# Second layer of a two-layer decoder: three stages issued one after the other, or in turns

## The chip, the core and the metric

The kernel runs on one core of a Trainium2 chip. The metric is the device time of one execution in microseconds (us). A core has engines that run side by side and each work off their own queue of instructions: TensorE (PE in the profile; its weight loads have a row of their own, PEld), VectorE (DVE), ScalarE (ACT), GpSimd (POOL), and SyncE (SP), which here only issues transfers. Matmul results land in PSUM, a memory of eight banks; VectorE and ScalarE read it, GpSimd doesn't in this kernel. Everything else lives in SBUF, with 128 partitions.

## What is computed

The input `x` is 64 sequences of 64 tokens with 256 features, so 4096 tokens; `ctx_512` gives 64 context vectors of 64 features for each sequence. There are two layers of three residual blocks, each behind a layer norm. The first layer (a state-space scan, an attention, a mixture of experts) stays as it is. The change is to the second:

```python
x = x + _L1_attn_ref(_layernorm(x), ...)             # recurrent mean ("wkv")
x = x + _L1_xattn_ref(_layernorm(x), ctx_512, ctx_512)   # grouped attention ("gqa")
x = x + _L1_ffn_ref(_layernorm(x), ...)              # grouped experts ("ffn")
```

The recurrent mean mixes each token with the one before it in three ways, multiplies by three matrices, and runs a recurrence along the 64 tokens of a sequence:

```python
mfo = max(mx, kt + tf);  e1 = exp(mx - mfo);  e2 = exp(kt + tf - mfo)
out = (e1 * num + e2 * vt) / (e1 * den + e2)
mfs = max(mx + td, kt);  e1s = exp(mx + td - mfs);  e2s = exp(kt - mfs)
carry = (e1s * num + e2s * vt, e1s * den + e2s, mfs)
...
return sigmoid(rec @ Wr) * out @ Wo
```

The grouped attention has 32 query heads of 8 features over 8 key-value heads, within one sequence. The grouped experts choose 8 of 64 small experts for each token, gather their weights in 8 groups, add a mask term to the input of each group, and apply a gated pair of matrices (256 to 176) and one back (176 to 256) for each group; the eight results are summed.

No token depends on a token of another sequence, so all three stages can be done for one part of the sequences before another part is begun.

## The kernel before

The 4096 tokens are 8 blocks (`NBLK`) of 512 tokens (`TB`), which is 8 sequences (`NB`) or 4 tiles (`NT`) of 128 tokens. `x_sb` holds all of `x` in SBUF, 32 tiles of 128 x 256, and every stage adds its result to it in place. `run` goes through six phases, each over all 8 blocks: state-space scan, attention, experts, recurrent mean, grouped attention, grouped experts. Each phase has its own weight pool, work pool and PSUM pool; the pools lie in turn on the left and the right side of SBUF, so that the next phase's weights are loaded while one phase runs.

`phase` (L1114) is the loop of the last three phases: the front of a block is a function or a generator cut into pieces by `yield`; the items of a block then pass through a list of stages, each one step behind the one before, so that the stages of different items overlap. The order in which the program makes its instructions is what the queues start from. A framework then sorts them into the engines' queues and adds the waits; VectorE, ScalarE and GpSimd may get an instruction whose inputs are there ahead of an earlier one that still waits.

- Collecting (L696, `moe_collect`). The experts of the first layer leave two rows for each token in memory; an indirect transfer that GpSimd issues adds 128 rows to one tile of `x_sb`, 8 such transfers for a block. Blocks 0 and 1 are collected after the expert phase, the others one by one during the recurrent mean.
- Recurrent mean. `wkv_front` (L728): statistics of the layer norm, the norm on GpSimd (L106), transposes (L115), difference to the previous token (`wk_d`, L742), three mixes (`wk_mix`, L748), three projections into PSUM tiles of two banks (L755), copies and a sigmoid on ScalarE. `wkv_scan` (L766): three scans along the tokens on VectorE (L783, L801, L802), the exponents between them on VectorE, GpSimd and ScalarE, a reciprocal (`wk_dn`, L807), and the closing products on GpSimd (L808 to L812). `wkv_out` (L815): the output matrix and the addition to `x_sb`. All of it works on whole blocks: 128 partitions x (2 halves of the features x 512 tokens). Two PSUM tiles of two banks and four of one bank are in use.
- Grouped attention. `gqa_front` loads the context and lays it out for keys and values; `gqa_queries`, `gqa_max`, `gqa_turn`, `gqa_weights`, `gqa_values`, `gqa_out` treat one tile of 128 tokens each. All eight banks form one ring (tag `mm`).
- Grouped experts. `ffn_front` (9 pieces; L1012 to L1064): norm, transposes, the router matmul (`pl`), softmax, the largest 8, transposed weights (`weT`), the gathered weights (`pf`), a second softmax over the members of a group (`fl`, `soft`), and its transpose `smT`. `prep_ffn` (L985) makes the mask term's matrix once. An item is half of the groups of one tile: `ffn_up` (four `gu` tiles of one bank each, L1078 and L1082, then Silu on ScalarE, L1086, and a product on VectorE, L1087), `ffn_turn` (transposes, L1099, L1100), `ffn_down` (L1108), the addition to `x_sb` and the transfer of the result out.

ScalarE evaluates a function from a table that is loaded before it. The recurrent mean uses Exp and Sigmoid, the grouped attention Exp, the grouped experts Silu, and Exp in their front.

Of the kernel before, what the change touches and what calls it, by code (L numbers as in the profile page):

```python
# [6 lines left out]
F32 = mybir.dt.float32  # L7
# [11 lines left out]
NB = TB // S  # L19
NBLK = 8  # L20
# [21 lines left out]
class Net:  # L42
# [28 lines left out]
    def mm(self, shape, name):  # L71

        return self.pp.tile(shape, F32, tag="mm", bufs=8 - 2 * self.n_big, name=name)
# [5 lines left out]
    def open_psum(self, n_big):  # L79
        self.n_big = n_big  # L80
        self.pp = self.tc.alloc_tile_pool(name="psum", bufs=1, space=PSUM, reuse_waits="tile")


    def stats(self, wk, blk):

        nc = self.nc
        st = wk.tile([P, NT, 6], F32, tag="ln_st", bufs=2, name="ln_st")
        mv = wk.tile([P, NT, 2], F32, tag="ln_mv", bufs=2, name="ln_mv")
        for t in range(NT):
            nc.vector.bn_stats(st[:, t], self.x[:, blk * NT + t])  # L90
            nc.vector.bn_aggr(mv[:, t], st[:, t])
        ve = wk.tile([P, NT], F32, tag="ln_ve", bufs=2, name="ln_ve")
        nc.vector.tensor_scalar(ve, mv[:, :, 1], LN_EPS, None, ALU.add)
        rs = wk.tile([P, NT], F32, tag="ln_rs", bufs=2, name="ln_rs")
        nc.gpsimd.tensor_tensor(rs, ve, self.mhalf, ALU.pow)
        return mv, rs

    def neg_mean_times(self, wk, mv, rs, tag="ln_nm"):
        nm = wk.tile([P, NT], F32, tag=tag, bufs=2, name=tag)
# [19 lines left out]
    def ln_T(self, wk, blk, eng):  # L119
        nc = self.nc  # L120
        mv, rs = self.stats(wk, blk)
# [59 lines left out]
    def ssm_front(self, wk, w, blk):  # L181
        nc, te = self.nc, self.nc.tensor
        mv, rs = self.stats(wk, blk)
# [287 lines left out]
    def moe_front(self, wk, w, b, f):  # L471
# [6 lines left out]
        mv, rs = self.stats(wk, b)  # L478
# [169 lines left out]
    def moe_phase(self, wk, w):  # L648
# [40 lines left out]
        for b in range(2):  # L689
            self.moe_collect(b)  # L690

    def moe_collect(self, b):

        for k in range(2):
            for i in range(NT):
                self.nc.gpsimd.indirect_dma_start(self.x[:, b * NT + i], None, self.ys,  # L696
                                                  bass.IndirectOffsetOnAxis(self.left[:, b, k, i:i + 1], 0), compute_op=ALU.add)


    def w_wkv(self, side):  # L700
# [12 lines left out]
        w["tdp"] = wp.tile([P, 2, NB, S + 1], F32, name="wkv_tdp")  # L713
# [6 lines left out]
    def wkv_padded(self, wk, n, fill, bufs=1):  # L720

        t = wk.tile([P, 2, NB, S + 1], F32, tag="wk_" + n, bufs=bufs, name="wk_" + n)
        t = t.rearrange("p c b s -> p (c b) s")
# [3 lines left out]
    def wkv_plain(self, wk, n, bufs=1):  # L727
        t = wk.tile([P, 2, TB], F32, tag="wk_" + n, bufs=bufs, name="wk_" + n)  # L728
        return t, t.rearrange("p c (b s) -> p (c b) s", s=S)

    def wkv_front(self, wk, w, blk):
        nc, te, v, gp = self.nc, self.nc.tensor, self.nc.vector, self.nc.gpsimd
        mv, rs = self.stats(wk, blk)
        nm = self.neg_mean_times(wk, mv, rs)
        h = self.norm(wk, blk, rs, nm, gp)
        ps = self.transposed(h)
# [515 lines left out]
```

## Time and profile before

| | us |
|---|---|
| median of 3 runs | 2495.43 |
| lowest and highest run | 2490.35, 2496.96 |
| the profiled execution, by its own clock | 2489.17 |
| its span, first to last instruction | 2487.4 |
| TensorE busy (share of the span) | 2061.0 (83%) |
| VectorE busy | 1243.2 (50%) |
| ScalarE busy | 720.4 (29%) |
| GpSimd busy | 857.1 (34%) |

Busy time is the union of an engine's instructions. A matmul's end is modelled, so a busy TensorE need not be at its peak; the distance from one matmul to the next is the better measure of what one costs. "PEclk" is the TensorE clock that was granted, as a share of the full one. All times on the axis are counted from the first instruction. A share over the whole span is a mean over six phases with different limits, so the phases have to be looked at one by one.

### The profile page before, as it was taken

What the parts mean: (1) busy time and instruction counts of PE and PEld (TensorE: products, weight loads), DVE (VectorE), ACT (ScalarE), POOL (GpSimd) and SP (SyncE); (2) the same over time, 40 slices, a digit from 0 to 9 for tenths busy, and PEclk for the clock granted to TensorE, in tenths of its full rate; (3) what the DMA queues carried; (4) which work ended last, traced back from release to release, by engine and by line L of the source; (5) the groups of instructions that cost most, each with busy time, mean ns of one, the idle gap of its engine ahead of it and who ended that gap; (6) DMA issues with size and microseconds to landing.
All of it is one profiled execution on the core that took longest, in us unless ns stands there. A gap on an engine that the chain in (4) does not pass through costs nothing.

```text
span 2487.4 us, 31746 instructions
## 1 busy us (share of the span) xinstructions
PE 2061.0 (83%) x12394; PEld 1447.3 (58%) x12394; DVE 1243.2 (50%) x2672; ACT 720.4 (29%) x1282; POOL 857.1 (34%) x1001
## 2 busy tenths in 40 slices
PE   6899998999999479999822353538997999999999
PEld 3566674666667367888711121225764666667666
DVE  5554657544345433333325599886875323332322
ACT  2232431222232343333202122214662222222221
POOL 4443354222221432011289967656632000000000
PEclk8898999999999579999966676668997999999999
DMA  4011009540000111677333100022000000000000
GB/s 131 30 30 30 1 1 283 177 124 5 1 5 8 60 55 55 218 237 237 116 52 46 26 0 0 0 74 57 13 3 1 9 7 7 9 7 9 7 7 11
DMA packets 109960, 133.78 MB, mean 54 GB/s; under 512 B 31850, under 2 KB 98546, under 8 KB 109810
## 3 DMA queue, kind: packets, MB, share of 16 engines
q1 hardware_dynamic: 94482, 104.48, 13.7%
q0 software_dynamic: 15328, 27.27, 4.4%
q8 instruction: 98, 1.61, 0.3%
q14 instruction: 52, 0.43, 0.1%
HBM read 75.23 MB, written 56.49 MB: 53 GB/s over the span
## 4 chain that ended last, share of the span: by engine, by line
PE 32%; issue 13%; POOL 10%; DVE 7%; DMA 0%; SPq 0%; ACT 0%; POOLq 0%; DVEq 0%; ACTq 0%
PE gu_ps L1078 12%; PE acc L1108 6%; POOL x_sb L696 4%; PE gu_ps L1082 2%; PE aT_ps L1099 2%; DVE wk_dn L807 2%; PE st L919 2%; DVE wk_mix L748 1%; PE sc L906 1%; PE pq L883 1%; PE pv L930 1%; POOL moe_ys L646 1%; POOL h L106 1%; POOL wk_o L812 1%; DVE wk_den L801 1%
## 5 line engine op out<-in xcount | busy, mean ns | idle before, releaser
L1078 PE MATMUL gu_ps<-ffn_gu,hT 128*128 128x352 f32 x1024 | 315.5, 461 | 0.0
L1078 PEld LDWEIGHTS gu_ps<-ffn_gu,hT 128*128 128x128 f32 x1024 | 192.4, 191 | 97.2 <-issue 0.8
L1087 DVE SCALAR_TENSOR_TENSOR a<-a,fr_sca,gu_ps 128x176 f32<-128x176 f32 x256 | 84.6, 393 | 308.3 <-ACT a L1086 308.3
L115 PE MATMUL hT_ps<-ident,h 128*128 128x128 f32 x192 | 41.7, 356 | 177.8 <-POOL h L106 151.4
L1108 PE MATMUL acc<-ffn_d,aT 128*128 128x256 f32 x704 | 162.4, 379 | 0.0
L1086 ACT ACTIVATE a<-gu_ps 128x176 f32<-128x176 f32 x256 | 60.5, 322 | 348.0 <-PE gu_ps L1082 348.0
L106 POOL TENSOR_SCALAR h<-x_sb,ln_rs,ln_nm 128x256 f32<-128x256 f32 x64 | 44.8, 798 | 300.6 <-PE hT_ps L1012 298.2
L209 PE MATMUL proj<-hT,w_in 128*128 128x512 f32 x320 | 145.8, 612 | 0.0
L115 PEld LDWEIGHTS hT_ps<-ident,h 128*128 128x128 f32 x192 | 29.6, 176 | 190.0 <-POOL h L106 162.0
L1108 PEld LDWEIGHTS acc<-ffn_d,aT 128*128 128x128 f32 x704 | 128.8, 190 | 14.9
L392 POOL TENSOR_TENSOR p<-p,sm 128x1024 f32<-128x1024 f32 x32 | 60.9, 1902 | 186.1 <-DVE sm L391 186.1
L628 DVE TENSOR_TENSOR gT<-gT,uT 128x512 f32<-128x512 f32 x54 | 37.4, 692 | 166.9 <-ACT gT L627 166.9
L413 PE MATMUL po<-xa_vo,ctxT 128*128 128x256 f32 x512 | 117.6, 379 | 0.0
L696 POOL DMA_INDIRECT x_sb<-moe_ys,left x64 | 109.7, 1714 | 20.1 <-issue 19.8
L373 PE MATMUL q_ps<-hT,xa_q 128*128 128x512 f32 x256 | 113.8, 602 | 1.5 <-ACT hT L126 1.4
L413 PEld LDWEIGHTS po<-xa_vo,ctxT 128*128 128x128 f32 x512 | 96.3, 190 | 25.8 <-issue 12.2
L646 POOL DMA_DIRECT2D moe_ys<-y x38 | 27.2, 717 | 238.3 <-DVE y L645 231.3
L209 PEld LDWEIGHTS proj<-hT,w_in 128*128 128x128 f32 x320 | 61.4, 196 | 71.7 <-issue 68.6
L90 DVE BATCH_NORM_STATS2 ln_st<-x_sb 128x6 f32<-128x256 f32 x192 | 75.1, 405 | 42.2 <-DMA x_sb<-moe_ys,left 37.3
L755 PE MATMUL pk<-wk_mix,wkv_k 128*128 128x512 f32 x64 | 44.5, 850 | 54.5 <-DVE wk_mix L748 54.5
L254 POOL TENSOR_TENSOR ul<-ssm_U,la 128x512 f32<-128x512 f32 x32 | 34.1, 1067 | 156.8 <-PE pld L256 156.8
L540 POOL DMA_INDIRECT moe_hs<-moe_h,moe_slots x64 | 62.4, 974 | 73.5 <-issue 34.3
(324 smaller groups left out, 4587.8 us busy)
## 6 DMA issues: line engine op xcount, KB each, us to landing
moe_hs<-moe_zero SPq DMA_DIRECT2D x30, 1088.0 KB, 11.2
pack<-in_moe_pack_dram SPq DMA_DIRECT2D x38, 770.0 KB, 5.5
ht<-moe_hs SPq DMA_DIRECT2D x38, 272.0 KB, 2.8
moe_ys<-y POOLq DMA_DIRECT2D x38, 256.0 KB, 5.6
c<-in_ctx_dram SPq DMA_DIRECT2D x40, 128.0 KB, 3.0
x_sb<-in_x_dram SPq DMA_DIRECT2D x8, 512.0 KB, 7.3
out_dram<-x_sb SPq DMA_DIRECT2D x32, 128.0 KB, 1.7
ffn_gu<-in_ffn_guT_dram SPq DMA_DIRECT2D x8, 352.0 KB, 7.6
```

The lines of the kernel that those rows point to most:

```text
L90: nc.vector.bn_stats(st[:, t], self.x[:, blk * NT + t])
L106: eng.tensor_scalar(h[:, t], self.x[:, blk * NT + t], rs[:, t:t + 1], nm[:, t:t + 1], ALU.mult, ALU.add)
L115: self.nc.tensor.transpose(ps[:, t * P:(t + 1) * P], h[:, t, c * P:(c + 1) * P], self.ident)
L209: te.matmul(ps, w["in"][:, c, col:col + P], hT[:, c], start=c == 0, stop=c == 1)
L373: te.matmul(ps, wq[:, c, hp * P:(hp + 1) * P], hT[:, c], start=c == 0, stop=c == 1)
L392: nc.gpsimd.tensor_mul(p, p, bc(sm, 2, S))
L413: self.nc.tensor.matmul(po, st["cT"][:, hp], w["vo"][:, hp], start=hp == 0, stop=hp == 7)
L540: s = gp.indirect_dma_start(w["hs"], bass.IndirectOffsetOnAxis(w["slots"][:, b, k, i:i + 1], 0), ha[k][:, i], None).ins
L696: self.nc.gpsimd.indirect_dma_start(self.x[:, b * NT + i], None, self.ys, bass.IndirectOffsetOnAxis(self.left[:, b, k, i:i + 1], 0), compu ...
L1078: te.matmul(ps, f["hT"][:, c, tok], w["gu"][:, 4 * q + j, c], start=c == 0, stop=False)
L1087: v.scalar_tensor_tensor(a[:, e], a[:, e], f["sca"][:, k:k + 1], pg[j][:, 176:352], ALU.mult, ALU.mult)
L1108: self.nc.tensor.matmul(f["acc"][t], st["aT"][:, k], w["d"][:, k], start=k == 0, stop=k == 10)
```

## The change

The last three phases become one, `layer1`, with one PSUM pool: a ring of seven one-bank tiles (`n_mm = 7`) and one bank for the sums of `ffn_down` (tag `acc`). `beside` takes one piece at a time from several generators, in proportion to the numbers given with them, until all are done. After the recurrent mean of block 0 alone, and that of block 1 beside the attention of block 0, eight rounds follow: the grouped experts of block b, the recurrent mean of block b+2 (with the collecting of block b+3 ahead of it), and the grouped attention of block b+1 with the front of its experts behind it.

```diff
+        def wkv(b):
+            if b + 1 < NBLK:
+                yield from self.collect_block(b + 1)
+            if b < NBLK:
+                yield from self.wkv_block(wk, w_wkv, b)
+        def gqa(b):
+            if b < NBLK:
+                yield from self.gqa_block(wk, w_gqa, b)
+                yield from self.ffn_front(wk, w_ffn, b, fs[b])
+        def beside(*streams):
+            at = [0.0] * len(streams)
+            live = [iter(s) for s, _ in streams]
+            most = max(n for _, n in streams)
+            while any(x is not None for x in live):
+                for i, (_, n) in enumerate(streams):
+                    at[i] += n / most
+                    while at[i] >= 1 and live[i] is not None:
+                        at[i] -= 1
+                        if next(live[i], 1) is not None:
+                            live[i] = None
+        for _ in self.collect_block(0):
+            pass
+        beside((wkv(0), 1))
+        beside((wkv(1), 50), (gqa(0), 36))
+        self.prep_ffn(wk, w_ffn)
+        for b in range(NBLK):
+            beside((self.ffn_block(wk, w_ffn, b, fs), 40), (wkv(b + 2), 50), (gqa(b + 1), 40))
```

The recurrent mean works on half blocks (`HB`, 4 sequences, 2 tiles). `wkv_block` takes pieces of the scan of one half and of the front of the next half by turns. The norm moves from GpSimd to ScalarE, the projections use one bank each, the Sigmoid becomes an Exp whose 1 + e^-r is multiplied into the denominator, so that one reciprocal gives both, and many products overwrite their input:

```diff
-    def wkv_front(self, wk, w, blk):
+    def wkv_front(self, wk, w, n0, f):
...
-        h = self.norm(wk, blk, rs, nm, gp)
-        ps = self.transposed(h)
+        h = wk.tile([P, 2, D], F32, tag="wk_h", bufs=1, name="wk_h")
+        for t in range(2):
+            nc.scalar.activation(h[:, t], self.x[:, n0 + t], AF.Identity, bias=nm[:, t:t + 1], scale=rs[:, t:t + 1])
+        yield
+        ps = self.mm([P, 2 * HB, S], "wk_hT")
...
-            ps = self.big([P, 2, TB], "p" + n)
+            ps = self.mm([P, 2, HB * S], "p" + n)
...
-        nc.scalar.activation(r, proj("r", mixed(2))[0], AF.Sigmoid)
+        nc.scalar.activation(er, proj("r", mr)[0], AF.Exp, scale=-1.0)
...
-        gp.tensor_mul(ev[:, :, 1:], e2s[:, :, 1:], vs)
-        v.tensor_tensor_scan(flat(num), flat(e1s), flat(ev), 0.0, ALU.mult, ALU.add)
...
-        v.reciprocal(dn, dn)
-        gp.tensor_mul(ov, e1, num[:, :, :S])
-        gp.tensor_mul(e2, e2, vs)
-        gp.tensor_add(ov, ov, e2)
-        gp.tensor_mul(rv, rv, dn)
-        gp.tensor_mul(ov, ov, rv)
+        gp.tensor_mul(e2s[:, :, 1:], e2s[:, :, 1:], vs)
+        dn = den[:, :, :S]
+        v.tensor_mul(dn, dn, e1)
+        v.tensor_add(dn, dn, e2)
+        v.scalar_tensor_tensor(dn, er, 1.0, dn, ALU.add, ALU.mult)
+        yield
+        v.tensor_tensor_scan(flat(num), flat(e1s), flat(e2s), 0.0, ALU.mult, ALU.add)
+        gp.tensor_mul(e2, e2, vs)
+        yield
+        v.reciprocal(er, dn)
+        gp.tensor_mul(e1, e1, num[:, :, :S])
+        gp.tensor_add(e1, e1, e2)
+        yield
+        gp.tensor_mul(ov, e1, er)
...
+        v.tensor_add(self.x[:, n0:n0 + 2], self.x[:, n0:n0 + 2], po)
```

The pieces of the attention and of the experts come from generators of their own. The experts' pipeline runs on from one block to the next; `ffn_up` is cut between its second and third bank; `ffn_turn` takes small tiles of its own (three buffers); `ffn_front` has a cut more. To make room, many SBUF tiles have one buffer where they had two to four (context, keys, values, `soft`, the front's scratch), and the mask weights are loaded into a work tile in `prep_ffn`.

```diff
+        for k in range(b * n, (b + 1) * n + (len(stages) - 1 if b == NBLK - 1 else 0)):
+            for d, stage in enumerate(stages):
+                if 0 <= k - d < NBLK * n:
+                    c, i = divmod(k - d, n)
+                    yield from stage(wk, w, fs[c], c, i, self.fst[k - d])
...
-            f["acc"][t] = self.mm([P, D], "acc")
+            self.acc = self.pp.tile([P, D], F32, tag="acc", bufs=1, name="acc")
...
+        w[5] = self.w_ffn("left")
+        self.open_psum(0)
+        self.n_mm = 7
+        wk = self.pool("work3", "left")
+        self.layer1(wk, w[3], w[4], w[5])
```

The weights of the recurrent mean and of the attention are loaded, and the attention's tiles cleared on GpSimd, before the first layer's experts instead of after them; the grouped experts' weights follow right behind those experts.

## The prediction

> **What bounds the kernel now.** First the busy times by stage, in stretches of time that I cut where one phase hands over to the next (length, then busy us and instructions of each engine, the granted clock, the transfers' share, GB/s):
>
> ```profile
> core 0: us, PE busy (x) PEld busy (x) DVE busy (x) ACT busy (x) POOL busy (x), PEclk, DMA share, GB/s
> 1231.00:1268.00 37.00, 2.83 (x14) 2.14 (x12) 7.95 (x20) 0.00 (x0) 31.66 (x32) 0.60 0.40 57
> 1268.00:1674.00 406.00, 169.86 (x384) 87.64 (x384) 291.97 (x242) 87.39 (x89) 308.88 (x208) 0.67 0.14 23
> 1674.00:1690.00 16.00, 2.41 (x10) 2.16 (x11) 9.22 (x50) 1.09 (x2) 11.38 (x33) 0.54 0.88 213
> 1690.00:1870.00 180.00, 174.85 (x3512) 123.15 (x3510) 138.46 (x282) 106.98 (x199) 97.59 (x301) 0.99 0.07 15
> 1870.00:1895.00 25.00, 10.39 (x40) 8.20 (x41) 17.88 (x86) 2.00 (x4) 11.01 (x17) 0.50 0.00 0
> 1895.00:2487.40 592.40, 589.12 (x2874) 408.74 (x2872) 173.51 (x524) 146.60 (x385) 13.90 (x23) 1.00 0.02 8
> ```
>
> The second layer takes half of the span, from 1231 on. Its recurrent mean (second row) needs TensorE for a part of its 406 us, at 0.67 of the clock; VectorE and GpSimd carry it. Attention (fourth row) and experts (last) are TensorE's alone; GpSimd has nearly nothing to do beside the experts. The two kinds of stage run one after the other.
>
> Then the groups of the recurrent mean's stretch, to see what its cadence is made of (busy us, mean ns of one, idle before it and who ended it):
>
> ```profile
> L748 DVE SCALAR_TENSOR_TENSOR wk_mix<-wk_d,wkv_vec,wk_hp 128x512 f32<-128x512 f32 x48 | 55.6, 1208 | 34.2 <-POOL wk_d L742 31.7 <-PE pk L755 2.5
> L807 DVE RECIPROCAL wk_dn<-wk_dn 128x1024 f32<-128x1024 f32 x8 | 52.3, 6540 | 0.0
> ...
> L812 POOL TENSOR_TENSOR wk_o<-wk_o,wk_r 128x1024 f32<-128x1024 f32 x8 | 29.1, 3635 | 0.6
> ...
> L801 DVE TENSOR_TENSOR_SCAN wk_den<-wk_e1s,wk_e2s 128x1040 f32<-128x1040 f32 x8 | 24.4, 3044 | 5.8 <-ACT wk_e1s L797 5.8
> ```
>
> In the chain of waits the long reciprocals begin at 1420.09, 1451.10, 1492.31, 1536.81, 1577.88, 1622.29 and 1654.92: 39 us a block.
>
> Last, TensorE in order of time where the experts' first front stands alone:
>
> ```profile
> 1875.91 3.25 PE L1018 MATMUL pl<-ffn_r,hT 128*128 128x64 f32 x14 [1.04 <-DVE hT L1013]
> 1885.17 1.06 PE L1036 MATMUL weT_ps<-ident,fr_sc 128*64 128x128 f32 x4 [6.01 <-DVE fr_sc L1032]
> 1886.90 1.97 PE L1042 MATMUL pf<-ffn_at,fr_weT 64*128 64x64 f32 x8 [0.67 <-ACT fr_weT L1038]
> 1894.15 1.11 PE L1062 MATMUL smT_ps<-ident,ffn_soft 128*128 128x128 f32 x4 [5.29 <-DVE ffn_soft L1057]
> 1895.06 5.27 PE L1078 MATMUL gu_ps<-ffn_gu,hT 128*128 128x352 f32 x14
> ```
>
> The `gu` matmuls need `hT`, which the `pl` matmuls before them had read, and all PSUM was free; yet they stand behind `smT_ps`. TensorE keeps the order of issue when an input is late. VectorE doesn't: in the same 25 us its row has 86 instructions, most of them layer-norm statistics of later blocks slipped in between. This decides what the turns can hide.
>
> **What the skill says.** "Perfetto Trace Analysis", Optimization Strategy, says that where the most-contended engine changes over time, interleaving those regimes may help: rows two and six are such a pair. "ScalarE: Activation LUTs", What ACT_TABLE_LOAD costs, gives about 1283 ns for a change of function set plus a drain; the trace's loads take 1283 ns each, and it shows no separate drain. "SBUF — State Buffer", Who interferes with whom, says that a VectorE instruction with two SBUF inputs and a GpSimd instruction that reads SBUF block each other whole; here the 48 mixes average 1208 ns, while their median is 740, so it agrees. "TensorE: Matmul & The Clock Gate", Part 1, has the clock halved when TensorE idles; the rows agree (0.50 where it waits, 1.00 where it doesn't).
>
> **The change, part by part.** All times count against the profiled execution: 2489.17 us, of which 2487.4 is the span and 1.8 lies around it; the median of the runs is 6.3 above it.
>
> *TensorE's work.* It is nearly the same, now at full clock. Experts: 1895.06 to the last addition's start at 2484.2, 589 us, of which a whole block with its front takes 74.1 (`gu` groups at 1973.82 and 2047.91 in the chain). Attention: 174.9 less 11.05 for `mgu` is 163.8, 20.5 a block. Recurrent mean, a block: 48 projection matmuls of 256 columns at 0.231 (row L1108, 162.4/704), 16 of the output at the same, 8 transposes at 0.149 (L1099, 52.4/352): 11.1 + 3.7 + 1.2 = 16.0. A full round needs 74 + 20.5 + 16 = 110.5 us.
>
> *The other engines in a round.* VectorE: recurrent mean, each half 6 mixes, 6 exponent steps at 0.42 (256 columns, row L131), 3 scans at 1.2 and a reciprocal at 3.3 (halves of 2.31, the shortest scan, and 6.54), 4 products of 512 at 0.68, statistics 1.3, so 16 and 32 a block; attention 138.5/8 = 17; experts 173.5/8 = 22. Sum 71, and by the stretch that the recurrent mean shows (292 busy where its durations at their minimum sum to about 219) up to 95. GpSimd: 16 products of 512 at 1.07 (L254), 8 collects at 1.85, attention 97.6/8 = 12, norm 3: 47. ScalarE: attention 13, experts 18, recurrent mean 12, and table loads: by the turns Silu and Exp change about 10 times a round, against two or three loads a block in the experts now: 10 x 1.28 = 13, sum 56. All lie beside 110 of TensorE. Nothing is lost on them unless TensorE waits for one.
>
> *The lead-in.* Collecting ends 1246 for block 0 and 1261 for block 1, for these 16 transfers come first on GpSimd; now 17 clearing instructions, which move ahead of the experts, come before the first `rs` (1268.5). I take 1262. First half of block 0, alone: front 10 us, scan 19 (the durations above in a row), done at 1291; each further half by the cadence of 39 us a block plus fixed costs, 21: 1312 for block 0 and 1354 for block 1. The attention of block 0 fits beside it (20.5 of TensorE). Of the front behind it some 18 of the 23.7 us that it takes now (1871.41 to 1895.06) stick out: 1372. `mgu` 11: experts start at 1383 (bounds 1368 to 1405), not at 1895.
>
> *The end of a round.* Counting pieces: experts have 32 in a round, each taking 0.8 of a turn, so they end in turn 40; the recurrent mean has 42 and a last one; attention and front have 37, ending in turn 47. The last five, from behind `pl` to `smT`, therefore stand with no TensorE work beside them but one `po` (1.8 us), and TensorE doesn't pass over them: 15.9 us from the end of `pl` to `gu` in the fence above. Less the statistics that slip in (about 2) and the matmuls that I have counted already (3.6), plus VectorE pieces of the recurrent mean in the way (a reciprocal, 3.3 at most) and a cold clock (the 14 `gu` took 5.27 instead of 4.2): 14 a round, in seven rounds 98. Bounds 4 (if the pieces are pulled ahead) and 20.
>
> *Waits inside a round.* One bank less, and three streams that draw on seven. A `gu` set of four is held until Silu and product are through; with a table load this is about 1.28 + 0.94 + 0.4 later; attention asks for four banks eight times a round, three of them right behind a `gu` set. The trace of before has no such mixture: its attention waits 1.2 us in all, its experts nothing. At least 0, at most some 25 a round; I take 2 us for five such places, 10 a round in six rounds and 5 in the one without a recurrent mean: 65 in all.
>
> *Nothing else.* Weights of the experts (4.2 MB) now load from about 1235, when their space comes free, 140 us ahead of use; context loads keep one buffer, free a round ahead. Costing SP's queue at nothing rests on that. The norm on ScalarE instead of GpSimd is 4 x 0.6 a block, under TensorE.
>
> *Sum.* 1383 + 589 + 6 x 16 + 7 x 20.5 + 98 + 65 = 2374.5, with 3 us to the span's end and 1.8 around it 2379: 110 less than 2489.17. Against the median 2495.43 that is **2385 us**.
>
> **Rivals.** *TensorE hardly waits* (0.15): the tails cost 4 and the waits 3 a round, 98 - 28 + 65 - 20 = 115 less: 2270. For it: 592 us of experts without a gap, with the front's pieces among the items. Against: there an item of 9 us lay between two pieces, here a third of it and, at the end, nothing.
>
> *The small engines set the pace* (0.13): VectorE at 95, with ScalarE's loads in its inputs, can't keep the order that TensorE needs, and rounds take 150 instead of 135: 6 x 15 more, 2475. For it: the stretched rows of L748 and L801. Against: GpSimd is at half, not three quarters, of a round. If the queues are sorted otherwise than the turns ask (the statistics above show that they are sorted), it ends here or at the first rival.
>
> *Slower* (0.12): the bank ring. Of 16 four-bank requests a round (8 `gu`, 8 of attention) each makes TensorE wait for a table load and a VectorE instruction ahead of the release. 110 of gain and 65 granted already are 175 over about 6.5 rounds, 27 a round, 1.7 us a request: from there the change loses. At 2.2, which is 1.28 and one 0.9 of VectorE, it is 35 a round, 230 in place of 65: 2550. For it: each place has this wait on its way. Against: three of the seven banks are usually free, and only a few sets follow each other closely.
>
> **Numbers.** My case has 0.60, with 2320 to 2450 as its own range by the bounds of lead-in, tails and waits. The range over the cases is 2290 to 2475: it leaves out the slow case and most of the fastest. Faster by over 0.3% (which is what a measurement of this kernel can tell from none) 0.87, the same 0.01, slower 0.12.
>
> **What would show it.** Right: TensorE's share of the span up from 83% to near 87%; `gu` first at 1370 to 1400; six rounds of 125 to 145; at the end of each a gap on TensorE of 10 to 15 ended by `sc`, `weT` and `soft`, the clock down there; table loads from 72 to over 100; reciprocals at half of 6.5. Wrong: gaps before `gu` or `sc` ended by `a`, L1087, in every set (the ring), or VectorE above 80% in the rounds.

## The result: 0.4% faster, and where the rest stayed

| | before | after |
|---|---|---|
| median of 11 runs each, side by side | 2492.94 us | 2485.05 us |
| ratio, with its 95% interval | | 0.9963 (0.9951 to 0.9974) |
| profiled execution, span | 2487.4 us | 2483.3 us |
| first `gu` matmul of the experts | 1895.1 us | 1498.7 us |
| TensorE's share of the span | 83% | 84% |
| loads of ScalarE's function tables | 72 | 106 |

The change gains 8 us where 110 were forecast. The profiled execution took 2485.1, of which 1.8 lies around the span, against 2379 in the forecast's sum. The whole difference lies in one place. The busy times by stage of the changed kernel (columns as in the first view of the prediction; rows left out are rounds like those shown):

```profile
1231.00:1385.00 154.00, 35.72 (x112) 26.36 (x110) 49.86 (x106) 17.09 (x30) 134.65 (x120) 0.61 0.52 96
1385.00:1460.00 75.00, 50.90 (x511) 34.60 (x511) 58.32 (x110) 26.87 (x49) 45.76 (x73) 0.80 0.03 7
1460.00:1498.70 38.70, 23.52 (x79) 16.84 (x79) 17.55 (x41) 3.86 (x6) 14.01 (x24) 0.60 0.00 1
...
1626.10:1762.60 136.50, 116.48 (x873) 81.54 (x873) 80.52 (x169) 53.23 (x102) 44.10 (x73) 0.93 0.03 8
1762.60:1901.40 138.80, 118.98 (x874) 83.13 (x873) 80.81 (x165) 53.23 (x102) 42.82 (x73) 0.91 0.03 8
...
2296.10:2404.50 108.40, 99.13 (x802) 67.60 (x802) 41.29 (x107) 39.93 (x80) 7.65 (x14) 0.96 0.02 6
2404.50:2483.30 78.80, 75.58 (x346) 51.65 (x345) 15.73 (x42) 13.73 (x43) 0.00 (x0) 0.97 0.03 9
```

The first three rows are the lead-in, up to the first `gu`. It was to end at 1383 and ends at 1498.7, 116 us later. TensorE has 110 us of work in these 268, at 0.61, 0.80 and 0.60 of its clock; in the first row GpSimd is busy for 135 of 154 us. The fourth and fifth rows are full rounds, of 136.5 and 138.8 us; the last two are the round without a recurrent mean and the experts' last block. From the first `gu` to the end of the span it takes 984.6 us; the forecast had 994.5. So the rounds came out as forecast, to 10 us in the sum, and the lead-in took all the gain. In part the sum is luck: the four full rounds took 134.7 to 138.8 us, 2 more on average than the 134.5 that the terms give, while the first round (127.4) and the sixth (123.0) were shorter.

The groups of the recurrent mean, all blocks together (columns as before):

```profile
L828 DVE RECIPROCAL wk_er<-wk_den 128x512 f32<-128x512 f32 x16 | 53.5, 3343 | 0.2
...
L752 DVE SCALAR_TENSOR_TENSOR wk_mix<-wk_d,wkv_vec,wk_hp 128x256 f32<-128x256 f32 x96 | 44.9, 519 | 37.9 <-POOL wk_d L745 25.5 <-PE pk L759 12.3
...
L833 POOL TENSOR_TENSOR wk_o<-wk_e,wk_er 128x512 f32<-128x512 f32 x16 | 20.9, 1307 | 26.1 <-DVE fr_s L1038 10.6 <-PE wk_po L839 10.0 <-DVE wk_er L828 5.5
```

Each half's reciprocal takes 3343 ns against 6540 for a whole block, and the mix of 256 columns 519 instead of 1208 for 512. The pieces themselves are as short as they were to be.

TensorE in order of time at the end of a round (start, us, then the matmuls, and in brackets idle time and who ended it):

```profile
1589.02 3.19 PE L1127 MATMUL acc<-ffn_d,aT 128*128 128x256 f32 x14
1592.04 1.89 PE L759 MATMUL pk<-wk_mix,wkv_k 128*128 128x256 f32 x8
...
1607.97 1.89 PE L1127 MATMUL acc<-ffn_d,aT 128*128 128x256 f32 x8
1613.14 0.62 PE L1050 MATMUL weT_ps<-ident,fr_sc 128*64 128x128 f32 x4 [3.28 <-DVE ln_mv L92]
1614.43 1.96 PE L1056 MATMUL pf<-ffn_at,fr_weT 64*128 64x64 f32 x8 [0.67 <-ACT fr_weT L1052]
1625.18 1.09 PE L1076 MATMUL smT_ps<-ident,ffn_soft 128*128 128x128 f32 x4 [8.78 <-DVE ffn_soft L1071]
1626.06 2.56 PE L1093 MATMUL gu_ps<-ffn_gu,hT 128*128 128x352 f32 x4
```

The experts' last matmuls of the round are at 1589 and 1608; after that TensorE has `weT`, `pf` and `smT` of the next front to do and nothing else to do beside them, and from 1610 to 1626 it works for less than 4 us. This is the gap that the prediction put at the end of each round.

### The profile page after: what moved, and what is told of

Same layout as the page of the kernel before. It is cut to its first block, busy times and chain, and to the rows that moved or that the text cites. A ratio compares the mean times of both kernels' runs of the same rounds, so it can differ in the third digit from the quotient of the medians.

```text
span 2483.3 us, 32529 instructions
## 1 busy us (share of the span) xinstructions
PE 2084.7 (84%) x12586; PEld 1494.0 (60%) x12586; DVE 1242.7 (50%) x2832; ACT 782.6 (32%) x1404; POOL 832.6 (34%) x1047
## 4 chain that ended last, share of the span: by engine, by line
PE 40%; DVE 9%; POOL 8%; ACT 3%; issue 2%; DMA 1%; POOLq 0%; DVEq 0%; ACTq 0%
PE gu_ps L1093 11%; PE acc L1127 5%; PE u_ps L618 3%; PE g_ps L627 3%; PE d_ps L638 3%; POOL x_sb L693 3%; PE gu_ps L1099 2%; PE st L933 1%; PE sc L920 1%; PE aT_ps L1115 1%; POOL fr_h L1020 1%; DVE wk_er L828 1%; PE pv L944 1%; PE pq L897 1%; PE pr L759 1%
## 5 line engine op out<-in xcount | busy, mean ns | idle before, releaser
L1093 PE MATMUL gu_ps<-ffn_gu,hT 128*128 128x352 f32 x1024 | 338.8, 478 | 0.0
L1127 PEld LDWEIGHTS acc<-ffn_d,aT 128*128 128x128 f32 x704 | 129.6, 191 | 21.8 <-issue 6.5
L414 PEld LDWEIGHTS po<-xa_vo,ctxT 128*128 128x128 f32 x512 | 96.3, 190 | 25.8 <-issue 12.2
L693 POOL DMA_INDIRECT x_sb<-moe_ys,left x64 | 103.8, 1621 | 18.8 <-issue 17.3
L909 POOL TENSOR_SCALAR gqa_q<-x_sb,ln_rs,ln_nm 128x64 f32<-128x64 f32 x128 | 54.6, 445 | 136.4 <-PE pq L897 134.6
L922 DVE TENSOR_REDUCE gqa_q<-sc 128x8 f32<-128x512 f32 x128 | 79.4, 683 | 13.0 <-PE sc L920 12.0
L374 PEld LDWEIGHTS q_ps<-hT,xa_q 128*128 128x128 f32 x256 | 48.4, 192 | 61.5 <-issue 55.6
L618 PE MATMUL u_ps<-htT,pack 128*128 128x256 f32 x304 | 78.1, 379 | 0.0
L627 PE MATMUL g_ps<-uT,pack 128*128 128x256 f32 x304 | 78.0, 379 | 0.0
```

Of the source, the lines that this page charges most:

```text
L374: te.matmul(ps, wq[:, c, hp * P:(hp + 1) * P], hT[:, c], start=c == 0, stop=c == 1)
L414: self.nc.tensor.matmul(po, st["cT"][:, hp], w["vo"][:, hp], start=hp == 0, stop=hp == 7)
L618: nc.tensor.matmul(ps[:, m], m_[:, c, m * P:(m + 1) * P], st["hT"][:, c], start=c == 0, stop=c == 1)
L627: nc.tensor.matmul(ps[:, m], m_[:, c, m * P:(m + 1) * P], st["uT"][:, c], start=c == 0, stop=c == 1)
L922: v.tensor_reduce(st["qa"][:, :, k, 16:18], sc[k], AX.X, ALU.max, negate=True)
L1093: te.matmul(ps, f["hT"][:, c, tok], w["gu"][:, 4 * q + j, c], start=c == 0, stop=False)
```

## What the trace shows of the lead-in

Two lines, first of the kernel before and then of the changed one, on the transfers by which GpSimd collects the first layer's expert outputs (shortest, median and longest in ns, first and last start):

```profile
L696 POOL DMA_INDIRECT x_sb<-moe_ys,left x64: 1531/1549/3555, 1231.7 to 1403.3; - x64
```

```profile
L693 POOL DMA_INDIRECT x_sb<-moe_ys,left x64: 1530/1556/2483, 1233.0 to 1382.1; - x64
```

There are eight a block, so 64. In the program, the changed kernel issues those of block b+1 with the recurrent mean of block b; but the order of GpSimd's queue is laid out ahead of the run, and there all 64 stand early, probably since a transfer waits for nothing late. They run from 1233 to 1384, beside the recurrent mean of the first block. What that does to a half block is seen on GpSimd (columns as in the view of TensorE above), first in the changed kernel:

```profile
1288.63 1.85 POOL L794 TENSOR_TENSOR wk_e2s<-wk_k,wk_mx 128x512 f32<-128x512 f32 x1
1290.64 1.55 POOL L693 DMA_INDIRECT x_sb<-moe_ys,left  x1 [0.16 <-issue]
1291.64 1.75 POOL L800 TENSOR_TENSOR wk_e<-wk_e,wk_mx 128x512 f32<-128x512 f32 x1
...
1307.50 1.78 POOL L818 TENSOR_TENSOR wk_e2s<-wk_e2s,wk_v 128x512 f32<-128x512 f32 x1
...
1321.51 1.75 POOL L829 TENSOR_TENSOR wk_e<-wk_e,wk_num 128x512 f32<-128x512 f32 x1
...
1342.42 1.57 POOL L693 DMA_INDIRECT x_sb<-moe_ys,left  x1 [0.30 <-issue]
1344.30 1.57 POOL L693 DMA_INDIRECT x_sb<-moe_ys,left  x1 [0.30 <-issue]
1345.92 1.26 POOL L833 TENSOR_TENSOR wk_o<-wk_e,wk_er 128x512 f32<-128x512 f32 x1
```

From the first product of this half, `wk_e2s` at 1288.63, to its last, `wk_o`, it takes 57 us, and between them there is one transfer behind another, 1.85 us apart. The line of the kernel before says the same of that kernel: its transfers ran until 1403, and its first two blocks took until 1420, where the second of the long reciprocals begins. The first begins at 1361.4:

```profile
1361.38 6.54 DVE L807 RECIPROCAL wk_dn<-wk_dn 128x1024 f32<-128x1024 f32 x1
```

The prediction listed the reciprocals from 1420 on, read 39 us a block from them, and carried this cadence to the first two blocks. The lines on these two blocks were in the trace. That the transfers stretch a half block is so far only seen beside them; the runs below move them or leave them out.

## The experiments

The times of the kernel before differ a little from session to session (medians of 2486.9, 2490.1, 2495.3 and 2494.9 us), so kernels are compared by the ratio of each to the kernel before in the same session. The changed kernel's is 0.9963; 0.001 is 2.5 us. Unless said otherwise, a kernel is the changed kernel with one edit.

### Are the collects the cost? `hold` and `b_hold`

`hold` keeps the transfers of blocks 2 to 7 behind a product of the recurrent mean:

```diff
-        gp.tensor_mul(ov, e1, er)
+        self.last = gp.tensor_mul(ov, e1, er).ins
...
-                self.moe_collect(b, k, i)
+                with self.tc.issue_after(self.last):
+                    self.moe_collect(b, k, i)
```

> The changed kernel, with the collecting transfers of blocks 2 to 7 kept behind the last product of the recurrent mean issued before them. Theory A (collects): in the changed kernel GpSimd issues all 64 collects between 1233 and 1384, 1.85 us each, and the 48 of blocks 2 to 7 (89 us) stand between the products of the first two recurrent means. Held back, 40 or more of them leave that stretch: the first gu moves from 1499 to 1410-1425 and the time from 2485 to 2395-2415; the rounds stay at about 135 us, with 15 us more on GpSimd. Theory B (chain): the four half blocks take what their own chain of engines takes, and the collects only fill GpSimd's idle time: gu moves by less than 25 us, time above 2460. Theory C (given back): gu moves, but the collects then delay GpSimd's products in the rounds: rounds of 145 and more, time 2450-2490.

Measured: 1.005 (1.003 to 1.007), slower than both kernels. The first `gu` came at 1458.7, 40 us earlier, and the first half block was out at 1296 instead of 1347. But the four rounds that now had collects in them took 139, 154, 151 and 152 us, against 127, 137, 139 and 135 in the changed kernel; the next one, without, took 137 as before. Theory C holds in its mechanism, and the time is above its 2490: the rounds lost more than the lead-in got back. GpSimd in the first round of `hold`:

```profile
1528.80 1.64 POOL L693 DMA_INDIRECT x_sb<-moe_ys,left  x1 [0.16 <-issue]
...
1541.82 1.54 POOL L693 DMA_INDIRECT x_sb<-moe_ys,left  x1 [0.31 <-issue]
1542.81 1.30 POOL L959 TENSOR_TENSOR x_sb<-x_sb,at 128x256 f32<-128x256 f32 x1
```

The eight transfers stand in one row, 14 us long, and the attention's addition (L959) comes behind them, at 1542.81. In the same stretch TensorE waited 10.2 us before its `po` transposes.

`b_hold` makes the same edit in the kernel before:

> The kernel before, with the collects of blocks 2 to 7 held behind the last product of the recurrent mean before them, as in hold. Theory A (collects): its first two blocks took 59 and more against 39-42 of the later ones (reciprocals at 1361, 1420, then 1451, 1492), so the first two are quicker by 60-80, but each later block has 15 us more on GpSimd in a cadence that GpSimd and VectorE share: 20-60 us gained, 2430-2475. Theory B (chain): less than 10 gained, or slower. In either case less than hold gains.

Measured: 1.004 (1.0026 to 1.0054). Its first two blocks are quicker (reciprocals at 1312 and 1346 instead of 1361 and 1420), the later ones slower, and the last begins at 1659 as against 1655. Theory A has the place right and the gain wrong: here, where GpSimd and VectorE set the pace, moving GpSimd's work gained nothing.

### What the collects cost at most: `no_collect`

```diff
-            if b + 1 < NBLK:
+            if b == 0:
                 yield from self.collect_block(b + 1)
```

> The changed kernel without the collects of blocks 2 to 7: their tokens don't get the first layer's expert outputs added. What the collects cost at most, wherever they are put. If they cost the lead-in alone: first gu at 1410-1430, rounds as in the changed kernel (137), time 2395-2420. If the lead-in is mostly the half blocks' own chain: gu at 1450 or later.

Measured: 0.9689 (0.9671 to 0.9707), 68 us below the changed kernel. The first half block on GpSimd:

```profile
1267.73 1.28 POOL L794 TENSOR_TENSOR wk_e2s<-wk_k,wk_mx 128x512 f32<-128x512 f32 x1 [1.00 <-DVE wk_mx L788]
1269.77 1.35 POOL L800 TENSOR_TENSOR wk_e<-wk_e,wk_mx 128x512 f32<-128x512 f32 x1 [0.76 <-DVE wk_e L798]
...
1277.37 3.17 POOL L818 TENSOR_TENSOR wk_e2s<-wk_e2s,wk_v 128x512 f32<-128x512 f32 x1 [3.28 <-DVE ffn_at L988]
...
1289.54 1.18 POOL L829 TENSOR_TENSOR wk_e<-wk_e,wk_num 128x512 f32<-128x512 f32 x1
...
1292.13 1.26 POOL L833 TENSOR_TENSOR wk_o<-wk_e,wk_er 128x512 f32<-128x512 f32 x1
```

The same row of products, 24 us long instead of 57. The first `gu` comes at 1435.1, or 207.8 us behind the first collect, where the changed kernel has 265.7. The collects thus cost the lead-in 58 us. The rest of the gain is in the rounds (133 instead of 137): probably since the recurrent mean starts earlier in a round, without the collects' eight turns. But the lead-in isn't at 1383 yet; 58 us are still unexplained here.

### Is it the row of eight? `spread` and `spread2`

`spread` issues the collects one at a time, behind different products of the recurrent mean two blocks earlier:

```diff
+                for k, _ in enumerate(self.wkv_block(wk, w_wkv, b)):
+                    if b + 2 < NBLK and k % 5 == 4 and k < 40:
+                        with self.tc.issue_after(self.last):
+                            self.moe_collect(b + 2, *divmod(k // 5, NT))
+                    yield
```

> The changed kernel with each collect of blocks 2 to 7 issued singly, behind one of the recurrent mean's GpSimd products of two blocks earlier (one every five pieces), instead of eight in a row. Theory A (burst): in hold eight collects in a row kept GpSimd's queue 14-16 us, at 1319 and 1384 and once a round, and TensorE stood behind it; single ones delay a product by 1.85 us at most. First gu at 1430-1445, rounds back to 135-139, time 2415-2440. Theory B (every microsecond of GpSimd counts): rounds stay at 145-152 as in hold, time 2470-2500.

Measured: 0.9875 (0.9855 to 0.9896), but a recurrent mean has 34 pieces, so only six of each eight transfers were issued: two tiles of each of the blocks 2 to 7 lack their second expert output. Its time is not that of the whole work. `spread2` has one transfer every four pieces, and all of them:

> As spread, but with all eight collects of each block (spread issued six of them): one every four pieces of the recurrent mean two blocks earlier. Collects out of the lead-in are worth at most 58 there (first gu at 1441 in no_collect, on the changed kernel's origin, against 1499). Theory A (burst): first gu at 1455-1465, full rounds no longer than the changed kernel's 137, time 2440-2465. Theory B (every microsecond of GpSimd counts in a round): rounds of 145 and more, 2485-2500.

Measured: 0.996 (0.9947 to 0.9974), the time of the changed kernel. The lead-in is 39 us shorter (226.8 from the first collect to `gu`), and the rounds with collects take 143 to 146. Theory B holds. Against `no_collect`, whose recurrent mean has the same pieces at the same turns, such a round is 12.8 us longer (146.1 to 133.3), for 8 x 1.85 = 14.8 us of transfers on an engine that is busy for 58 of 146. Why an idle engine's time costs so much is seen on VectorE and TensorE in one of these rounds of `spread2`:

```profile
1780.85 0.88 DVE L807 SCALAR_TENSOR_TENSOR wk_e<-wk_k,wkv_vec,wk_e 128x256 f32<-128x256 f32 x2 [4.43 <-POOL wk_e L800]
...
1785.13 0.43 DVE L91 BATCH_NORM_STATS2 wn_st<-x_sb 128x6 f32<-128x256 f32 x1 [2.63 <-DMA x_sb<-moe_ys,left]
1785.48 1.30 DVE L1104 SCALAR_TENSOR_TENSOR a<-a,fr_sca,gu_ps 128x176 f32<-128x176 f32 x4
```

```profile
1776.75 0.93 PE L1115 MATMUL aT_ps<-ident,a 128*128 128x128 f32 x7
1785.91 1.65 PE L759 MATMUL pv<-wk_mix,wkv_v 128*128 128x256 f32 x3 [8.23 <-DVE a L1104]
```

VectorE's first wait here (the 4.43 in brackets) is for a product behind a transfer on GpSimd. Its second is for a transfer to land: the statistics of a later block (`wn_st`), which had been put in early, wait 2.6 us for the data, and behind them in VectorE's queue stand the experts' products `a`, which release the PSUM banks that TensorE's `pv` matmuls need. TensorE stood for 8.2 us. The prediction said of VectorE that it doesn't keep the order of issue when an input is late. That holds for the order in the program, which is changed before the run; the queue that came of it was kept here: VectorE stood still before `wn_st`, and four `a` followed without a further wait. The 40% of GpSimd in use says nothing of this; the wait passes through the queue of another engine. TensorE's waits ended by `a` come to 42 us in the four rounds with collects and to 15 in four rounds of `no_collect`; that is about half of what these rounds are longer, and the other half wasn't traced.

### The other 58 us of the lead-in: `nc_apart`

`no_collect`, with attention and front of block 0 behind the recurrent mean of block 1 instead of beside it:

```diff
-        beside((wkv(1), 50), (gqa(0), 36))
+        beside((wkv(1), 1))
+        beside((gqa(0), 1))
```

> no_collect (the tokens of blocks 2 to 7 don't get the first layer's expert outputs added) with the recurrent mean of block 1 issued alone, and attention and front of block 0 behind it instead of beside it. Theory A (attention beside slows it): the half blocks of block 1 come at 22 us, as those of block 0; its last output at 1360 instead of 1381; attention then 27 alone, front 20-24, mgu 11: first gu at 1418-1425 (no_collect: 1435). Theory B (block 1 is slow by itself): its half blocks stay at 29-36, and first gu comes 20 or more later, at 1455-1465. The rounds don't change.

Measured: 0.9708 (0.9681 to 0.9735), no better than `no_collect`. The first output matmul of a half block, and the first `gu`, each with the first collect put at 1233.0:

| | block 0, half 1 | half 2 | block 1, half 2 | first `gu` |
|---|---|---|---|---|
| forecast (done by) | 1291 | 1312 | 1354 | 1383 |
| changed kernel | 1347 | 1385 | 1459 | 1499 |
| `no_collect` | 1299 | 1321 | 1387 | 1441 |
| `nc_apart` | 1299 | 1321 | 1364 | 1447 |

Half blocks alone come at 21 to 22 us, as forecast; beside attention they take 29 to 36. That is theory A, but its gain of 10 or more isn't there: attention alone then needs the time that it no longer shares. From 1364 to 1447 it is 83 us for the attention of one block, a front and `mgu`, which the forecast had at 29, since it counted the attention's 20.5 us of TensorE as hidden beside block 1. Nor was it all hidden where it stood beside. TensorE in `no_collect`, from the last output of block 1 on (on its own axis, 5.6 us behind the table's):

```profile
1380.88 1.97 PE L839 MATMUL wk_po<-wkv_o,wk_o 128*128 128x256 f32 x8 [0.74 <-ACT pT L936]
...
1390.64 1.11 PE L954 MATMUL po<-ident,oT 128*128 128x128 f32 x4 [6.21 <-DVE oT L947]
1402.69 2.93 PE L1026 MATMUL hT_ps<-ident,fr_h 128*128 128x128 f32 x8 [10.93 <-POOL fr_h L1020]
...
1423.12 12.20 PE L1003 MATMUL mgu_ps<-ffn_gu,ffn_mu 128*128 128x352 f32 x32
```

Attention ends 11 us behind that output, the front takes 31 us more, and `mgu` 12. In `nc_apart`, alone and from a cold start, the attention of one block goes through its six stages one behind another and takes from 1370 to about 1410.

### The half blocks alone: `no_turns`

Half blocks, pieces and seven banks as in the changed kernel, but all recurrent means first, then all attention, then the experts:

> The changed kernel's half blocks, pieces and seven banks, but the stages one after the other as in the kernel before: all recurrent means, then all attention, then all experts with the next front beside. It prices the half blocks alone. By the prediction's steps a half block took 21 us, so eight blocks 340: time within 20 of the kernel before apart from attention's pipeline, filled anew in each block (8 x 5): 2490-2550. If a half block has nearly the chain of a whole block (27-36 us seen in hold): eight blocks 440-570, time 2570-2700.

Measured: 1.0244 (1.0226 to 1.0261), 2549.6 us, at the upper end of the first reading. Two stages of it, once the collects are over:

```profile
1385.00:1690.00 305.00, 162.83 (x473) 120.55 (x474) 285.76 (x343) 73.41 (x129) 178.35 (x182) 0.73 0.00 0
1690.00:1922.00 232.00, 201.86 (x3511) 134.07 (x3510) 151.01 (x342) 107.10 (x200) 104.34 (x309) 0.97 0.05 12
```

Fourteen halves in 305 us are 21.8 each; the forecast's 21 was right, and 43.6 a block is some 5 more than the 39 of whole blocks. Attention takes 232 instead of 180; its pipeline is filled anew in each block, and whether that makes up all of the 52 us wasn't tried. Against this version the turns gain 2.7%: they work, but first they have to pay for the cutting up.

### The end of a round: `tail`, `hold_tail`, `spaced`

`tail` changes the weights of the three streams, so that the experts last to the end of a round:

```diff
-            beside((self.ffn_block(wk, w_ffn, b, fs), 40), (wkv(b + 2), 50), (gqa(b + 1), 40))
+            beside((self.ffn_block(wk, w_ffn, b, fs), 33), (wkv(b + 2), 50), (gqa(b + 1), 47))
```

> The changed kernel, with the turns weighted 33 (experts), 50, 47 (attention and front) instead of 40, 50, 40, so that the experts last to the end of a round and the front's last pieces have them beside. Theory A (tail): at a round's end TensorE does 12 us of work in 34 (1592 to 1626), 20-22 lost a round; two thirds of it goes, 14 x 7 = 100: rounds of 115-120, time 2380-2410. Theory B (pace): VectorE and the chain of the front pace the round anyway, the waits move into the round: rounds of 130 and more, less than 30 us gained. Neither moves the first gu (1499).

Measured: 0.9938 (0.9922 to 0.9955), 6 us better than the changed kernel; full rounds of 134 to 139. That is theory B's time. The soft weights `smT` still cost TensorE up to 7.1 us a round, and `hT` up to 3.1: the matmuls beside are there, but TensorE keeps its order, and the piece that needs the late result comes too soon behind the one that starts it. With `hold` added:

> Both edits of hold and tail. If the two losses are separate, the gains add: 2485 - 80 - 100 = 2305, within 20. If the rounds come to be paced by GpSimd and VectorE once the tail is filled, the sum falls short by 40 or more.

Measured: 1.0002 (0.9991 to 1.0012). Its four rounds with collects are 11 to 14 us longer than those of `tail`, the longest 151.5, so the gains don't add.

`spaced` puts empty turns between the front's last pieces, so that other work is issued between a result's start and its use:

```diff
         v.tensor_mul(sc, sc, bc(s1, 2, S))
         yield
+        yield
+        yield
...
-            beside((self.ffn_block(wk, w_ffn, b, fs), 40), (wkv(b + 2), 50), (gqa(b + 1), 40))
+            beside((self.ffn_block(wk, w_ffn, b, fs), 33), (wkv(b + 2), 46), (gqa(b + 1), 50))
```

and likewise 2 behind the choice of eight, 1 behind `weT`, 3 behind `pf`, 2 behind the soft weights.

> The changed kernel with ten empty turns put between the front's last pieces (2 behind pl, 2 behind the choice of eight, 1 behind weT, 3 behind pf, 2 behind the soft weights) and weights 33, 46, 50, so that work of the experts and the recurrent mean is issued between them. In tail each round still waited 5-7 us for the soft weights and 3 for fr_h. Theory A (distance): TensorE's idle time of a full round falls from 20 us (changed kernel) and 14 (tail) to 8 or less, rounds of 118-126, time 2385-2430. Theory B (pace): as in tail, the waits move to other places and a full round stays at 132 or more; time 2455-2475.

Measured: 0.9686 (0.967 to 0.9703), 2411 us, 69 below the changed kernel. Two full rounds:

```profile
1742.00:1865.00 123.00, 113.62 (x873) 79.41 (x873) 77.36 (x166) 50.50 (x100) 41.69 (x74) 0.97 0.03 9
1865.00:1987.90 122.90, 113.55 (x872) 79.34 (x872) 76.13 (x160) 50.51 (x100) 41.65 (x74) 0.97 0.03 9
```

123 us, with TensorE busy for 113.6 and its clock at 0.97, and `weT`, `pf` and `smT` hardly waited for. First TensorE's longest waits in four full rounds of the changed kernel (total us, times, longest), then in four rounds of `spaced`:

```profile
PE weT_ps L1050 <- DVE ln_mv L92: 36.2, 4, 9.1
PE smT_ps L1076 <- DVE ffn_soft L1071: 17.8, 4, 4.5
PE pr L759 <- DVE a L1104: 7.7, 4, 1.9
PE hT_ps L1026 <- DVE a L1104: 6.2, 4, 1.6
...
PE pf L1056 <- ACT fr_weT L1052: 2.7, 4, 0.7
...
PE hT_ps L1026 <- POOL wk_hp L720: 2.1, 4, 0.6
```

```profile
PE hT_ps L1026 <- POOL fr_h L1020: 19.1, 7, 5.6
PE gu_ps L1103 <- DVE a L1114: 5.8, 4, 1.4
```

In the first fence the waits of `weT`, `smT` and `hT` make up 60 of the 80 us that TensorE was idle. The VectorE instruction named for `weT` is a statistic that had slipped in next to the front's own last one. In the second, those of `weT` and `smT` are gone. Theory A holds: the distance was missing, not the work. The weights of the streams changed too, and these weights alone weren't run; in `tail`, with weights near to them and no empty turns, full rounds stayed at 134 to 139.

### Banks and table loads: `ring6`, `plain_act`, `spaced_tanh`

The prediction charged the rounds with 65 us of waits on PSUM banks and table loads. `ring6` takes one more bank away (`self.n_mm = 6`):

> The changed kernel with six instead of seven PSUM banks in the shared set. The prediction charged the set of banks and the table loads with 65 us of waits inside the rounds. If banks bind there, one fewer costs 30 or more: 2515 and above. If TensorE waits for the front's chain alone, as the trace of the changed kernel shows, less than 12: below 2497.

Measured: 0.9979 (0.997 to 0.9987), 4 us more than the changed kernel. Its full rounds take 137 us, as with seven: one bank fewer doesn't bind.

`plain_act` replaces `AF.Silu` by `AF.Identity` in the experts:

> The changed kernel with Silu replaced by Identity, so that the gate isn't bent; the function sets change less often. If table loads make TensorE wait in the rounds (the prediction's 65 us), 25 or more are gained: below 2460. If they lie beside TensorE's work: within 10 of the changed kernel.

Measured: 0.9841 (0.9824 to 0.9859), 30 us less; full rounds of 129 instead of 137. Of the 80 loads of the second layer 79 are gone, so one costs on average 0.4 us of its 1.28. Most of it is at the end of the round: the four full rounds are 29 us shorter together, and TensorE waits 34 us in them for `weT`, `pf` and `smT`, where the changed kernel waits 57. `spaced_tanh` takes them away and keeps the gate, by half of x (1 + tanh(x / 2)); the Trainium skill, "ScalarE: Activation LUTs", Table sets, lists Tanh in the set of Exp, and the trace agrees, with one load left in the second layer, for its first Exp, where `spaced` has 74:

```diff
-            nc.scalar.activation(a[:, e], pg[j][:, 0:176], AF.Silu)
+            nc.scalar.activation(a[:, e], pg[j][:, 0:176], AF.Tanh, scale=0.5)
+            v.scalar_tensor_tensor(a[:, e], a[:, e], 1.0, pg[j][:, 0:176], ALU.add, ALU.mult)
```

> spaced, with x * sigmoid(x) as half of x * (1 + tanh(x / 2)): one more VectorE product of 176 columns for each set of gate columns (256 x 0.39 = 100 us more on VectorE over all blocks, 12.5 a round), no change of function set beside Exp if Tanh shares its set. Theory A (loads): ScalarE loses 79 x 1.28 = 101 us of loads, 12 a round, and the time falls by 15-30 against spaced: 2380-2396. Theory B (VectorE): VectorE's 12.5 a round stand in every PSUM set's release and cost as much or more: 2410-2450.

Measured: 0.9738 (0.971 to 0.9766), 13 us slower than `spaced`. Theory B: the extra product on VectorE costs more than the loads gave.

### Putting parts together: `best2`, `spaced_lead`

`best2` joins `spaced` and `spread2`, and reorders the lead-in:

> spaced and spread2 together, with the turns of a round weighted 33, 40, 50; and in the lead-in the mask weights' product (mgu, 11 us) moved behind the first recurrent mean, and attention and front of block 0 weighted 55 against 34 of the recurrent mean beside them. If the parts are separate: 2411 (spaced) - 40 (collects) - 11 (mgu) - 10 (front of block 0 earlier) = 2350; full rounds of 123, first gu at 1435-1445. If the collects in the rounds disturb the spaced order as they did in hold_tail (2488 against 2470 of tail): 2400 or more.

Measured: 0.978 (0.9764 to 0.9797), 23 us worse than `spaced` alone. The lead-in is 52 us shorter, and full rounds take 140 instead of 123. The weights of the streams differ too, so these 17 us aren't the collects' alone.

`spaced_lead` leaves the collects where they are:

```diff
+        self.prep_ffn(wk, w_ffn)
-        beside((wkv(1), 50), (gqa(0), 36))
-        self.prep_ffn(wk, w_ffn)
+        beside((wkv(1), 42), (gqa(0), 55))
```

> spaced, with the mgu product (11 us of TensorE) moved behind the first recurrent mean, and attention and front of block 0 weighted 55 against 42 beside block 1. The mgu product alone: 11 less. If the front of block 0 stood bare behind block 1: another 10 to 20. Time 2380-2400 against 2411 of spaced; the rounds stay at 123. If mgu in its new place waits for its weights or holds attention's matmuls: 2405 or more.

Measured: 0.9648 (0.9619 to 0.9678), 2406.7 us: the fastest version that computes everything, 3.2% below the changed kernel. The lead-in is 18 us shorter than in `spaced`, of which the first round gives 12 back (126.9 instead of 115.1). The interval overlaps that of `spaced`, so this last step is likely, not certain.

## Why the prediction was wrong

**The lead-in failed**, the step that has the experts start at 1383. Its terms, against the table of `nc_apart`:

- "for these 16 transfers come first on GpSimd": all 64 came there. Cost 58 us (`no_collect`). The prediction had priced the transfers in the rounds, eight each, by their place in the program, and at nothing beside TensorE. Put there, they cost 12.8 us a round, and the time is that of the changed kernel (`spread2`).
- "First half of block 0, alone: front 10 us, scan 19": 8 us short, also without the collects.
- "The attention of block 0 fits beside it": it holds the recurrent mean up. Block 1 takes 65 us in place of 42, 23 more.
- "Of the front behind it some 18 ... stick out", and 11 for `mgu`: 54 in place of 29, 25 more: attention ends 11 behind block 1, the front takes 31 instead of 18, and `mgu` 12.

These are 58 + 8 + 23 + 25 = 114 of the 116. The first is shown by leaving the transfers out, the third by the half blocks with attention beside and apart, the fourth by the fence on `no_collect`. What the attention costs together could only be moved: apart, the third term is gone, the fourth longer, and the first `gu` 6 us later (`nc_apart`). Why the front takes 31 there isn't shown; 10.9 of it is the wait for its norm, `fr_h`.

**The cadence.** "39 us a block" is right for the blocks it was read from, and the 21 of a half block is confirmed (21.8 in `no_turns`). It isn't the cadence of the stretch to which it was applied.

**TensorE's work.** 110.5 us a round fits: full rounds show 115 to 119 at a clock of 0.91 to 0.94, and those of `spaced`, with the same matmuls, 113.6 at 0.97.

**The other engines.** VectorE at 71 to 95 (measured 78 to 81), ScalarE 56 (53), table loads over 100 (106): right, and each of them below TensorE's 117. GpSimd's 47 (42 to 44) fits by luck: 15 of the 47 are transfers, which these rounds don't have; with them it is busy for 58 (`spread2`). "Nothing is lost on them unless TensorE waits for one" is where the transfers' price went missing. The 47 are also a third of a round and not, as the second rival's "against" has it, half.

**The end of a round.** 14 us a round: in the four full rounds of the fence above, `weT`, `smT` and `pf` cost 57, so 14 a round. **Waits inside a round**, 10: the rest of TensorE's idle time there is 23, so 6 a round, of which under 5 are ended by `a`, which frees a bank. Some 6 more a round go to the clock, which at 0.91 to 0.94 makes the 110.5 us of matmuls 117; of this the forecast had about 1, in the cold clock of the round's end. The two terms together were 24, against 26. What they were made of was partly off: one bank fewer costs the rounds nothing (`ring6`), while table loads cost 30 in all (`plain_act`), most of it at the round's end. And of the recurrent mean's work on VectorE the term allowed for one reciprocal, 3.3 us; at the end of the round that ends at 1762.6, VectorE does 7.7 us of it between the front's pieces.

**The rivals.** "The small engines set the pace" has the nearest time, 2475, but not its reason: VectorE isn't short of time in the rounds, and rounds took 137, not 150. TensorE stood long behind VectorE inside a round only when the collects were put there. The bank ring shows in the under 5 us a round that `a` ended, not in the 27 from which the change was to lose.

**"Nothing else"** held for the weights and context loads, for which no engine waited in the second layer; the queue that mattered, GpSimd's, wasn't on that list.

## What to carry to other kernels

A cadence belongs to the stretch it was read from: before it is carried to the first blocks, list what else stands in each engine's queue there, and look at when it runs, not at where the program has it. In a queue that keeps its order, overlap is a matter of distance: between the piece that starts a slow result and the one that uses it there must be as much issued work as the result takes, and here ten empty turns, with other weights, gained 69 us where the change itself gained 8. The share of time in which a helper engine is busy doesn't say what moving work onto it costs; a transfer that another engine waits for holds up everything behind that wait in that engine's queue, as in `spread2`.

## What the runs showed of the hardware

- Eight collects of 128 rows that follow each other on GpSimd keep it for 14 us, 1.85 each (1.55 busy, `hold`); spread over a round in which GpSimd was idle for more than half, they cost the round 12.8 us (`spread2`).
- A load of a function table takes 1283 ns on ScalarE in the groups of both kernels, but only about 0.4 us of it reached the total, 30 us for 79 (`plain_act`). In the changed kernel's round from 1626 to 1762, ScalarE still waited for its input after nine of the twelve loads, for 0.4 to 7.4 us.
- TensorE's granted clock in the changed kernel's lead-in was 0.53 to 0.67 in the three stretches of 50 us from 1250 to 1400, with gaps of up to 29 us in them. The same 32 matmuls of `mgu` took 10.9 us at a clock of 0.87 in the changed kernel and 12.2 at 0.78 in `no_collect`: time and clock multiply to 9.5 in both.
